# Shared expert of four more blocks made behind a recurrence, and a fourth buffer for the context's tiles

## The chip, the cores and the metric

The kernel runs on one NeuronCore of a Trainium2 chip. The metric is the device time of one execution in microseconds (us). In what follows PE is TensorE (matmuls; PEld its weight loads), DVE is VectorE, ACT is ScalarE, POOL is GpSimd and SP is SyncE, which here only issues DMAs. All data is float32 unless said otherwise. A line number such as L109 is a line of the kernel before the change.

## The reference, cut to what matters

A block of four layers is computed over 16 sequences of 128 tokens with 256 features. Each layer is a mixing step with a residual and a feed-forward step with a residual. The change lies in layer 1:

```python
def step(carry, xs):                  # L1 mixing: a scan over the 128 positions
    r, state = carry
    qt, kt, vt = xs
    r = decay * r + kt * vt
    inp = (qt * r).reshape(B, D) @ Wi.T + bi
    gate = sigmoid(inp @ Wg.T + bg)
    blended = gate * state + (1.0 - gate) * inp
    state = tanh(blended @ A.T + inp @ Bm.T)
    return (r, state), state @ Wo.T + bo

def _moe_forward(x, ...):             # L1 feed-forward, on the layer norm of x
    probs = softmax(x @ router_w.T)   # 64 experts, 8 of them for each token
    ...                               # at most 128 tokens for each expert
    gu = x @ ws_gate_up               # the shared expert, for every token
    sg, su = gu[:, :SF], gu[:, SF:]   # SF = 192
    return routed + silu(sg) * su @ ws_down
```

The next layer's mixing steps need gates, keys and values of a second tensor, the context (`ctx_1024`, 16 x 128 x 256).

## The kernel before, in words

The program has four stretches. Layer 0 comes first (`l0_xattn`, `l0_rest`). Then `l1_steps` runs the recurrence of layer 1, one step for each of the 128 positions. Then `l1_ffn` runs the 64 routed experts in 32 pairs (`l1_experts`). Last, `l2_l3` runs layers 2 and 3.

**A step of the recurrence** is a chain through four engines: PE adds `pre` and 8 small products of `gate` with `wA` (both fp32, so 8 and 16 records in the profile) into a PSUM bank, ACT takes the tanh (`th`, L954), DVE transposes it into `state` (L956) and multiplies the next step's `gate` with it (L959), and PE goes on.

**Work beside the recurrence** fills the engines' idle time. `spread` is a small planner written by hand: it lays chains of parts, each with an engine, a cost in us and a due step, into the 128 steps, so that no engine gets more than `room` allows in one step. In the order of their rights these chains are:

- `l1_block(q)`, first list: for block q, which is 16 positions (two tiles of 128 tokens): the output product, residual, layer norm (`h`), the transposed features `ht` (`even`, L1087), the router, the eight best experts (`best`, `chosen`, `differ`) and sorting keys (`turn_chosen`, `keys`). Block q can begin at step 16q + 16. Block 7 comes behind the last step.
- `l1_early`: the first half of the search for each expert's tokens, on DVE.
- `side_work`: eight pairs of context tiles (`pair(p)`, begin at step 1 + 8p) are loaded by `ctx_pair` into buffers of the tag `c`, of which there are three, and become keys, values (`kvt`) and centred values (`va`, on POOL, L297) for the later layers; four groups become gates. Buffers rotate: the load of pair p waits until POOL has read the tile of pair p - 3.
- `shared`: the second list of `l1_block(q)`, for q = 0 to 5, six steps before the first list's end at the earliest, laid last of all. It is the shared expert of one block: `widen` (8 matmuls of 256 columns, 16 records), a tanh, two copies on ACT and three products on POOL for the silu, `narrow` (4 matmuls, 8 records), a copy on ACT, and `end` (POOL adds it to `x`, and a DMA writes the sum to `expert_sums[0]`, on SP's queue for q under 4 and on POOL's else).

Parts that the planner puts behind step 127 are issued after the loop, along with block 7, and those not needed for the keys are ordered behind `self.turned`, block 7's `turn_chosen` on PE.

**Behind the recurrence** `l1_ffn` makes the router's weights (`l1_weights`), then the shared expert of blocks 6 and 7 in one go (`l1_shared`: matmuls of 512 columns, a real Silu on ACT), then the rest of the search (`l1_slots`: 16 rounds of `max` and `match_replace` on DVE, L1399 and L1401, then a transpose on PE, L1405, and index arithmetic into `slot_tok`). `l1_experts` gathers each expert's tokens with an indirect DMA on POOL (`xg`, L1261), transposes and multiplies on PE, and adds the weighted result into DRAM with another indirect DMA on POOL (`sum`, L1318). The order of instructions on each engine outside pinned parts comes from a scheduler that works at compile time; on the chip each engine takes them in that order.

**Weights of the experts** lie in slots of 9 KB a partition, one for each pair of experts (1.18 MB by eight DMAs on SP). Fourteen slots are used in turn: `EARLY` = 3 in the pool `keep`, filled during the recurrence; `RING` = 7 in `wring`, whose memory is that of the recurrence's helper pools (`side`, `blocks`) once these are done with; `MORE` = 1 in a pool on the right side; and `OLD` = 3, again in `keep`, where the tables of `l1_tables` (`one`, `two`, `three`) lay before: logits and masks, keys, and the features `ht` of blocks 6 and 7 with the router's and the shared expert's weights.

The lines that the prediction follows:

```python
        shared = [(ends[q] - 6, blocks[q][1]) for q in range(6)]
...
        at = ep % (EARLY + RING + MORE + OLD)
        ring = EARLY <= at < EARLY + RING
        w = self.slot(None if ring else self.more if EARLY <= at < EARLY + RING + MORE else self.keep)
```

Of the kernel before, what the change touches and what calls it, by code (L numbers as in the profile page):

```python
# [9 lines left out]
F32 = mybir.dt.float32  # L10
# [18 lines left out]
NE, TOPK, CAP, F1 = 64, 8, 128, 96  # L29


EARLY, RING, MORE, OLD = 3, 7, 1, 3
AHEAD = 5
SLOT = 2304
ROW = D + NE


# [24 lines left out]
class Kernel:  # L62
# [145 lines left out]
    def side_work(self, pool):  # L208
# [18 lines left out]
        def pair(p):  # L227

            s = {}

            def begin():
                s["c"] = self.ctx_pair(p, 3)
                s["st"] = self.small.tile([P, 2, 6], F32, tag="st", name="st")
                s["mv"] = self.small.tile([P, 2, 2], F32, tag="mv", name="mv")

            def stats(i):
                nc.vector.bn_stats(s["st"][:, i], s["c"][:, i])

            def spread(i):
                nc.vector.bn_aggr(s["mv"][:, i], s["st"][:, i])  # L240
                if i:
                    s["r"] = self.rstd(s["mv"][:, :, 1], 2)

            def shift():
                s["less"] = self.small.tile([P, 2], F32, tag="less", name="less")
                nc.vector.scalar_tensor_tensor(s["less"], s["mv"][:, :, 0], -1.0, s["r"], ALU.mult, ALU.mult)

            def scale(i):
                if not i:
                    s["h"] = pool.tile([P, 2, D], F32, tag="h", name="h")  # L250
                nc.scalar.activation(
                    s["h"][:, i], s["c"][:, i], AF.Identity, bias=s["less"][:, i:i + 1], scale=s["r"][:, i:i + 1]
                )

            def turn():
                for c in range(2):
                    for i in range(2):
                        at = (c * 2 + i) * P
                        self.flip(bank["T"][:, at:at + P], s["h"][:, i, c * P:(c + 1) * P])

            def affine(c):
                if not c:
                    s["ct"] = pool.tile([P, 2, 2 * P], F32, tag="ct", name="ct")
                nc.scalar.activation(
                    s["ct"][:, c], bank["T"][:, c * 2 * P:(c + 1) * 2 * P], AF.Identity,
                    bias=self.pcol("cln_b", c), scale=self.pcol("cln_g", c),
                )

            def keys():
                for c in range(2):  # L270
                    self.mm(bank["K"][:, :2 * P], wk[:, c], s["ct"][:, c], c == 0, c == 1)

            def values():
                for bb in range(2):
                    at = 2 * P + bb * 64
                    for c in range(2):
                        self.mm(
                            bank["K"][:, at:at + 64], s["ct"][:, c, bb * P:(bb + 1) * P], wv[:, c], c == 0, c == 1
                        )

            def keep():
                kvt = pool.tile([P, 3 * P], F32, tag="kvt", name="kvt")
                nc.scalar.copy(kvt, bank["K"][:, :3 * P])
                load(out=self.kvt_d[p], in_=kvt)

            def mean():
                s["heads"] = s["c"].rearrange("p b (h d) -> p (b h) d", h=4)
                s["mean"] = self.small.tile([P, 8], F32, tag="mean", name="mean")
                nc.vector.tensor_reduce(s["mean"], s["heads"], AX.X, ALU.add)

            def share():
                nc.gpsimd.tensor_scalar(s["mean"], s["mean"], 1.0 / 64, None, ALU.mult)

            def less():
                va = pool.tile([P, 2, 4, 65], F32, tag="va", name="va", bufs=2)
                nc.gpsimd.memset(va[:, :, :, 64:65], 1.0)
                nc.gpsimd.tensor_tensor(  # L297
                    va[:, :, :, :64].rearrange("p b h d -> p (b h) d"), s["heads"],
                    s["mean"].unsqueeze(2).to_broadcast([P, 8, 64]), ALU.subtract,
                )  # L300
                load(out=self.va_d[p // 2, :, p % 2 * 2:p % 2 * 2 + 2], in_=va)

            return [
                ("SP", 0, begin, 5), ("DVE", 0.5, lambda: stats(0), 0), ("DVE", 0.5, lambda: stats(1), 0),
                ("DVE", 0.2, lambda: spread(0), 0), ("DVE", 0.4, lambda: spread(1), 2), ("DVE", 0.2, shift, 0),
                ("ACT", 0.55, lambda: scale(0), 0), ("ACT", 0.55, lambda: scale(1), 0), ("PE", 0.45, turn, 0, "+T"),
                ("ACT", 0.57, lambda: affine(0), 0), ("ACT", 0.57, lambda: affine(1), 0, "-T"),
                ("PE", 0.86, keys, 0, "+K"), ("PE", 0.45, values, 0), ("ACT", 0.5, keep, 0, "-K"),
                ("DVE", 0.7, mean, 0), ("POOL", 0.4, share, 0), ("POOL", 1.4, less, 0),
            ]  # L310
# [604 lines left out]
    def l1_steps(self, pool, rec, side, last_used):  # L915
# [13 lines left out]
        blocks = [self.l1_block(last_used, q) for q in range(8)]  # L929
        urgent = [(16 * q + 16, blocks[q][0], True) for q in range(7)]  # L930
        out, ends = self.spread(urgent)
        shared = [(ends[q] - 6, blocks[q][1]) for q in range(6)]
        search = [(ends[3] + 1, self.l1_early())]
        beside, _ = self.spread(urgent + search + self.side_work(side) + shared)

# [52 lines left out]
    def l1_tables(self):  # L988
# [8 lines left out]
        w["best"], w["keys"] = two[:, :P], two[:, :5 * P]  # L997
        w["early"], w["iota"] = two[:, 5 * P:9 * P], two[:, 9 * P:17 * P]
        w["val"] = two[:, 17 * P:].rearrange("p (t k) -> p t k", t=NB)
        w["ht"] = three[:, :1024].rearrange("p (c n) -> p c n", c=2)  # L1000
        w["router"] = three[:, 1024:1152].rearrange("p (c n) -> p c n", c=2)
        w["sgu"] = three[:, 1152:1920].rearrange("p (c n) -> p c n", c=2)
        w["sd"] = self.keep.tile([F1, 2, D], F32, name="wsd", bufs=1)
# [20 lines left out]
    def l1_block(self, pool, q):  # L1024
# [55 lines left out]
                    self.flip(bank["T"][:, at:at + P], s["h"][:, h, c * P:(c + 1) * P])  # L1080

        def even():
            if q < 6:
                s["ht"] = pool.tile([P, 2, 2 * P], F32, tag="htb", name="ht", bufs=3)
            else:
                s["ht"] = w["ht"][:, :, (q - 6) * 2 * P:(q - 5) * 2 * P]
            nc.scalar.copy(s["ht"], bank["T"].rearrange("p (c n) -> p c n", c=2))  # L1087

        def router():
# [55 lines left out]

        def end():
            nc.gpsimd.tensor_tensor(xs, xs, s["out"].rearrange("p (h d) -> p h d", h=2), ALU.add)
            queue = nc.sync if q < 4 else nc.gpsimd
            queue.dma_start(out=self.block_rows(self.expert_sums[0], q), in_=xs)

        return [
            ("POOL", 1.3, bias, 0), ("ACT", 0.57, lambda: begin(0), 0), ("ACT", 0.57, lambda: begin(1), 0), ("PE", 0.86, lambda: out(0), 0, "+A"),
# [34 lines left out]
    def l1_ffn(self):  # L1187

        self.right.close()
        with self.tc.issue_after(self.ring_dma.ins):
            self.open_late()
        self.more = self.open(self.mids, "more", MORE, side="right")
        with (
            self.tc.tile_pool(name="l1h", bufs=2, reuse_waits="tile") as hidden,
            self.tc.tile_pool(name="l1r", bufs=1, reuse_waits="tile") as scratch,
        ):
            self.l1_weights(scratch)  # L1200

            with self.tc.issue_after(self.turned.ins):
                self.l1_shared(hidden)
            slot_tok = self.l1_slots(scratch)
        self.l1_experts(slot_tok, self.rows, self.expert_sums)
        self.sums = self.expert_sums
# [16 lines left out]
    def l1_fetch(self, ep):  # L1223

        nc, ins = self.nc, self.ins
        at = ep % (EARLY + RING + MORE + OLD)
        ring = EARLY <= at < EARLY + RING
        w = self.slot(None if ring else self.more if EARLY <= at < EARLY + RING + MORE else self.keep)
        wgu = w[:, :16 * F1].rearrange("p (j c n) -> p j c n", j=2, c=2)
        wd = w[:, 16 * F1:16 * F1 + 2 * D].rearrange("p (j d) -> p j d", j=2)  # L1230
        wt = w[:, 16 * F1 + 2 * D:]
# [113 lines left out]
    def l1_shared(self, pool):  # L1345

        nc, w = self.nc, self.l0
        act = pool.tile([F1, 2, GT], F32, tag="act", name="act")
        for f in range(2):
            pg, pu = self.psum("mm"), self.psum("mm")  # L1350
            for ps, at in ((pg, f), (pu, f + 2)):
                for c in range(2):

                    self.mm(ps[:F1], w["sgu"][:, c, at * F1:(at + 1) * F1], w["ht"][:, c], c == 0, c == 1)
            nc.scalar.activation(act[:, f], pg[:F1], AF.Silu)
            up = pool.tile([F1, GT], F32, tag="up", name="up")
            nc.scalar.copy(up, pu[:F1])
            nc.gpsimd.tensor_tensor(act[:, f], act[:, f], up, ALU.mult)
        for q in (6, 7):
            po = self.psum("mm")  # L1360
            for h in range(2):
                at = ((q - 6) * 2 + h) * P
                for f in range(2):
                    self.mm(po[:, h * D:(h + 1) * D], act[:, f, at:at + P], w["sd"][:, f], f == 0, f == 1)
            xs = self.x[:, q:q + 9:8]
            o = pool.tile([P, 2, D], F32, tag="o", name="o")
            nc.scalar.copy(o.rearrange("p i d -> p (i d)"), po)
            nc.gpsimd.tensor_tensor(xs, xs, o, ALU.add)
            nc.gpsimd.dma_start(out=self.block_rows(self.expert_sums[0], q), in_=xs)

    def l1_weights(self, scratch):

# [846 lines left out]
```

## Time and profile before

| what | value |
|---|---|
| median of 3 runs | 1703.3 us (1701.97 to 1705.75) |
| the profiled execution's own time | 1708.4 us |
| its span, from first to last instruction | 1706.7 us |
| mean granted TensorE clock | 0.945 |
| PE busy | 1527.6 us, 90% |
| DVE busy | 916.3 us, 54% |
| ACT busy | 744.6 us, 44% |
| POOL busy | 465.7 us, 27% |
| recurrence, first tanh to last | 616.3 to 817.4 us |
| search on DVE behind it | 832.6 to 861.6 us |
| first and last gather, last scatter of the experts | 866.4, 1061.6 and 1084.0 us (starts) |

The shares are averages over stretches with different limits, so each stretch has to be read by itself. Times of rows are counted from the span's start. "Granted clock" is the share of full speed that the throttle gave TensorE.

### The profile page before, as it was taken

The page shows a single profiled execution, that of the slowest core. Times are in us where ns is not written, and L with a number is a line of the kernel's source. Part 1 is how long each engine was busy: PE and PEld are TensorE (multiplying, and loading weights), DVE is VectorE, ACT ScalarE, POOL GpSimd, SP SyncE. Part 2 cuts the span into 40 slices and gives each one's busy share as a digit, 9 for nine tenths or more (in the row PEclk, how much of TensorE's full clock was granted, in tenths as well). Part 3 has the DMA queues.
Part 4 walks back from the last instruction along what each step waited for, and adds up shares of the span by engine and source line. Part 5 has one row for each costly group of instructions (what it writes and reads, how often), then busy time and mean ns, then how long its engine had stood idle before and what let it go on. Part 6 is the DMA issues. An engine that isn't in the chain of part 4 may idle for free.

```text
span 1706.7 us, 30312 instructions
## 1 busy us (share of the span) xinstructions
PE 1527.6 (90%) x11743; PEld 1083.7 (63%) x11743; DVE 916.3 (54%) x2410; ACT 744.6 (44%) x2178; POOL 465.7 (27%) x454
## 2 busy tenths in 40 slices
PE   7999999999999988888749889248999999999998
PEld 5777776765444446655437667136777777777776
DVE  4555464556466634557733323367675665765632
ACT  1443343344434223433313323135656756756555
POOL 2001000002122321232547888411421421402211
PEclk9999999999999977999779999668999999999999
DMA  8000000100001112342379997750000100100000
GB/s 260 7 7 7 7 1 1 50 13 23 0 13 38 62 41 86 118 157 72 105 216 285 294 306 154 186 196 16 23 29 19 27 24 27 30 12 8 7 7 13
DMA packets 89120, 125.76 MB, mean 74 GB/s; under 512 B 17936, under 2 KB 65872, under 8 KB 88848
## 3 DMA queue, kind: packets, MB, share of 16 engines
q1 hardware_dynamic: 75024, 101.76, 18.8%
q0 software_dynamic: 12832, 20.72, 5.9%
q8 instruction: 93, 1.52, 0.4%
q10 hardware_dynamic: 1120, 1.34, 0.2%
q14 instruction: 51, 0.42, 0.1%
HBM read 95.21 MB, written 28.57 MB: 73 GB/s over the span
## 4 chain that ended last, share of the span: by engine, by line
PE 66%; DVE 15%; issue 7%; POOL 4%; ACT 3%; DMA 3%; another core or an unknown queue 1%; ACTq 0%; SPq 0%; POOLq 0%; DVEq 0%
PE ps_all L109 43%; PE ps_mm L109 12%; PE ps_av L109 2%; PE ps_sc L109 2%; POOL rstd L161 1%; PE ps_all L1998 1%; PE ps_tp L419 1%; PE ps_all L1570 1%; DVE st L1548 1%; DVE gate L959 1%; DVE h L1553 1%; PE ps_all L1271 1%; DVE state L956 1%; ACT e L408 1%
## 5 line engine op out<-in xcount | busy, mean ns | idle before, releaser
L161 POOL TENSOR_TENSOR rstd<-ve,nhalf 128x2 f32<-128x2 f32 (+1 forms) x81 | 60.4, 749 | 585.9 <-DVE ve L159 500.1
L1990 POOL TENSOR_TENSOR e<-e,rs 128x512 f32<-128x512 f32 x64 | 66.1, 1040 | 282.6 <-DVE rs L1989 266.9
L408 ACT ACTIVATE e<-ps_sc,nmax 128x128 f32<-128x128 f32 x256 | 89.9, 377 | 108.0 <-DVE nmax L404 108.0
L109 PE MATMUL ps_all<-xt,w 128*64 128x128 f32 (+1 forms) x1024 | 104.8, 290 | 18.2 <-DVE xt L120 8.1
L109 PEld LDWEIGHTS ps_all<-xt,w 128*64 128x64 f32 (+1 forms) x1024 | 92.9, 173 | 33.0 <-issue 12.0
L1318 POOL DMA_INDIRECT sum<-y,slot_tok x64 | 102.2, 1596 | 32.5 <-issue 14.5
L1987 ACT ACTIVATE e<-e,nmax 128x128 f32<-128x128 f32 x256 | 99.3, 391 | 12.1 <-DVE nmax L1978 11.5
L954 ACT ACTIVATE th<-ps_all 128x64 f32<-128x64 f32 x128 | 28.6, 223 | 128.6 <-PE ps_all L109 128.1
L956 DVE STREAM_TRANSPOSE state<-th 128x64 f32<-128x64 f32 x128 | 31.3, 245 | 83.4 <-ACT th L954 82.2
L109 PE MATMUL ps_all<-wA,gate 128*16 128x64 f32 x2032 | 61.9, 241 | 15.3 <-DVE gate L959 13.6
L1570 PE MATMUL ps_all<-ident,h 128*128 128x128 f32 x168 | 29.1, 299 | 47.3 <-DVE h L1553 36.5
L1261 POOL DMA_INDIRECT xg<-rows,slot_tok x64 | 63.5, 993 | 26.4 <-issue 13.7
L109 PE MATMUL ps_mm<-ht,wq 128*128 128x256 f32 x256 | 69.7, 396 | 0.0
L109 PE MATMUL ps_mm<-ctxt,wk 128*128 128x256 f32 x256 | 66.9, 385 | 0.0
L109 PE MATMUL ps_mm<-wu,mt 128*128 128x256 f32 x256 | 66.0, 391 | 0.0
L109 PE MATMUL ps_all<-ht,w3q 128*128 128x256 f32 x256 | 61.9, 391 | 0.7 <-ACT ht L1941 0.7
L165 DVE TENSOR_TENSOR x<-x,ps_all 128x256 f32<-128x256 f32 x32 | 13.3, 416 | 89.7 <-PE ps_all L109 89.7
L1553 DVE TENSOR_SCALAR h<-x,mv,rstd 128x256 f32<-128x256 f32 x112 | 45.5, 435 | 29.8 <-POOL rstd L161 29.1
L109 PE MATMUL ps_all<-ht,w3v 128*128 128x256 f32 x256 | 60.9, 381 | 0.0
L109 PE MATMUL ps_all<-ht,w3g 128*128 128x256 f32 x256 | 60.5, 379 | 0.0
L1570 PEld LDWEIGHTS ps_all<-ident,h 128*128 128x128 f32 x168 | 19.8, 148 | 63.1 <-DVE h L1553 31.0
L109 PEld LDWEIGHTS ps_all<-wA,gate 128*16 128x16 f32 x2032 | 38.4, 104 | 33.8 <-DVE gate L959 30.9
(390 smaller groups left out, 3767.3 us busy)
## 6 DMA issues: line engine op xcount, KB each, us to landing
w<-in_moe_gate_up SPq DMA_DIRECT2D x64, 384.0 KB
w<-in_moe_down SPq DMA_DIRECT2D x64, 96.0 KB
c_in<-in_ctx SPq DMA_DIRECT2D x16, 256.0 KB
sum<-zero SPq DMA_DIRECT2D x8, 512.0 KB
w<-in_moe_down SPq DMA_DIRECT2D x64, 64.0 KB
ysum<-sum SPq DMA_DIRECT2D x16, 256.0 KB
low<-tops SPq DMA_DIRECT2D x12, 256.0 KB
va_d<-va SPq DMA_DIRECT2D x8, 260.0 KB
```

Source lines behind the costliest of these rows:

```text
L109: i = self.nc.tensor.matmul(out, lhsT, rhs, start=start, stop=stop)
L161: nc.gpsimd.tensor_tensor(r, ve, self.nhalf[:, :n], ALU.pow)
L408: nc.scalar.activation(e[:, i], src[:, i], AF.Exp, bias=nmax[:, i:i + 1], accum_out=ssum[:, i:i + 1])
L419: self.nc.tensor.transpose(pt[:, i * P:(i + 1) * P], e[:, i], self.ident)
L954: tanh = nc.scalar.activation(th, ps[:, :64], AF.Tanh)
L956: nc.vector.transpose(state[:, :, at:at + 32], th.rearrange("p (c n) -> p c n", c=2))
L1261: nc.gpsimd.indirect_dma_start(out=x, out_offset=None, in_=rows, in_offset=bass.IndirectOffsetOnAxis(ap=slot_tok[:, e:e + 1], axis=0),)
L1318: nc.gpsimd.indirect_dma_start(out=sums[e % len(sums)], out_offset=bass.IndirectOffsetOnAxis(ap=slot_tok[:, e:e + 1], axis=0), in_=y, in_o ...
L1553: nc.vector.tensor_scalar(h[:, i], src[:, i], mv[:, i, 0:1], r[:, i:i + 1], ALU.subtract, ALU.mult)
L1570: self.nc.tensor.transpose(pt[:, at:at + P], h[:, i, c * P:(c + 1) * P], self.ident)
L1987: nc.scalar.activation(e[:, i], e[:, i], AF.Exp, bias=nmax[:, i:i + 1], accum_out=ssum[:, i:i + 1])
L1990: nc.gpsimd.tensor_tensor(e, e, rs.unsqueeze(2).to_broadcast([P, 4, P]), ALU.mult)
```

## The change

The shared expert stays beside the recurrence for blocks 0 and 1 alone (`BESIDE` = 2). Blocks 2 to 7 keep their features `ht` on chip, in pairs of blocks: blocks 2 and 3 and blocks 4 and 5 in a new table `four`, blocks 6 and 7 in `three` as before. `l1_shared` then makes the shared expert of the three pairs one after the other behind block 7, with the same instructions as before for one pair. Their sums are written by DMAs of POOL's queue. The table `four` takes a slot in `keep`, which becomes the slot of a pair of experts later: `OLD` goes from 3 to 4 and `MORE` with its pool goes away, so there are fourteen slots as before. The tag `c` of the context's tiles gets a fourth buffer.

```diff
-EARLY, RING, MORE, OLD = 3, 7, 1, 3
+EARLY, RING, OLD = 3, 7, 4
+BESIDE = 2
...
-                s["c"] = self.ctx_pair(p, 3)
+                s["c"] = self.ctx_pair(p, 4)
...
-        shared = [(ends[q] - 6, blocks[q][1]) for q in range(6)]
+        shared = [(ends[q] - 6, blocks[q][1]) for q in range(BESIDE)]
...
-        w["ht"] = three[:, :1024].rearrange("p (c n) -> p c n", c=2)
+        four = self.slot(self.keep)
+        w["hts"] = [t.rearrange("p (c n) -> p c n", c=2) for t in (four[:, :1024], four[:, 1024:2048], three[:, :1024])]
...
-            if q < 6:
+            if q < BESIDE:
                 s["ht"] = pool.tile([P, 2, 2 * P], F32, tag="htb", name="ht", bufs=3)
             else:
-                s["ht"] = w["ht"][:, :, (q - 6) * 2 * P:(q - 5) * 2 * P]
+                at = q % 2 * 2 * P
+                s["ht"] = w["hts"][(q - BESIDE) // 2][:, :, at:at + 2 * P]
...
-            queue = nc.sync if q < 4 else nc.gpsimd
-            queue.dma_start(out=self.block_rows(self.expert_sums[0], q), in_=xs)
+            nc.sync.dma_start(out=self.block_rows(self.expert_sums[0], q), in_=xs)
...
-        self.more = self.open(self.mids, "more", MORE, side="right")
...
-        at = ep % (EARLY + RING + MORE + OLD)
+        at = ep % (EARLY + RING + OLD)
-        w = self.slot(None if ring else self.more if EARLY <= at < EARLY + RING + MORE else self.keep)
+        w = self.slot(None if ring else self.keep)
...
     def l1_shared(self, pool):
-        act = pool.tile([F1, 2, GT], F32, tag="act", name="act")
-        for f in range(2):
+        for n, ht in enumerate(w["hts"]):
+            act = pool.tile([F1, 2, GT], F32, tag="act", name="act")
+            for f in range(2):
...
-        for q in (6, 7):
+            for q in (BESIDE + 2 * n, BESIDE + 2 * n + 1):
...
```

More of the change, by code (lines that the diff above doesn't have):

```diff
@@ L1347, in l1_shared @@
         nc, w = self.nc, self.l0
-        act = pool.tile([F1, 2, GT], F32, tag="act", name="act")
-        for f in range(2):
[L1350 to L1358, printed above, removed]
@@ L1359, in l1_shared @@
-        for q in (6, 7):
[L1360 to L1369, printed above, removed]
+        for n, ht in enumerate(w["hts"]):
+            act = pool.tile([F1, 2, GT], F32, tag="act", name="act")
+            for f in range(2):
+                pg, pu = self.psum("mm"), self.psum("mm")
+                for ps, at in ((pg, f), (pu, f + 2)):
+                    for c in range(2):
+                        self.mm(ps[:F1], w["sgu"][:, c, at * F1:(at + 1) * F1], ht[:, c], c == 0, c == 1)
+                nc.scalar.activation(act[:, f], pg[:F1], AF.Silu)
+                up = pool.tile([F1, GT], F32, tag="up", name="up")
+                nc.scalar.copy(up, pu[:F1])
+                nc.gpsimd.tensor_tensor(act[:, f], act[:, f], up, ALU.mult)
+            for q in (BESIDE + 2 * n, BESIDE + 2 * n + 1):
+                po = self.psum("mm")
+                for h in range(2):
+                    at = (q % 2 * 2 + h) * P
+                    for f in range(2):
+                        self.mm(po[:, h * D:(h + 1) * D], act[:, f, at:at + P], w["sd"][:, f], f == 0, f == 1)
+                xs = self.x[:, q:q + 9:8]
+                o = pool.tile([P, 2, D], F32, tag="o", name="o")
+                nc.scalar.copy(o.rearrange("p i d -> p (i d)"), po)
+                nc.gpsimd.tensor_tensor(xs, xs, o, ALU.add)
+                nc.gpsimd.dma_start(out=self.block_rows(self.expert_sums[0], q), in_=xs)
```

## The prediction

> **What bounds the kernel now.** I read the page's chain first, then the four stretches that the change touches. A difference under 0.2% (3.4 us) is about what a measurement of this kernel can't tell from none.
>
> The recurrence. The tile view of `th` gives its ends: 127 intervals in 201.1 us, 1.58 on average. The timeline of ACT's tanh gives single steps: a bare step takes 1.27 us, one with a burst of four records of the shared expert 1.49 to 1.53. The windows view has the clock of three stretches of it:
>
> ```profile
> L954 ACT ACTIVATE th<-ps_all x128: 223/223/224, 616.3 to 817.4; 128x64 f32<-128x64 f32 x128
> ```
> ```profile
> core 0: us, PE busy (x) PEld busy (x) DVE busy (x) ACT busy (x) POOL busy (x), PEclk, DMA share, GB/s
> 616.00:619.00 3.00, 1.77 (x56) 0.89 (x56) 0.88 (x4) 0.66 (x3) 0.00 (x0) 1.00 0.00 0
> 619.00:638.00 19.00, 13.80 (x329) 7.09 (x329) 6.78 (x33) 3.71 (x15) 0.72 (x1) 0.51 0.01 3
> ...
> 768.00:813.00 45.00, 39.08 (x868) 24.93 (x866) 33.96 (x127) 15.39 (x55) 12.25 (x11) 1.00 0.21 68
> ...
> 858.00:878.00 20.00, 5.10 (x19) 3.91 (x20) 6.36 (x19) 0.00 (x0) 9.76 (x12) 0.51 0.97 288
> ```
>
> The number behind POOL's is the granted clock (PEclk): half in 619 to 638, where almost nothing runs beside the steps, full in 768 to 813, where bursts do. The last row has the DMA engines at 0.97 while the first tokens are gathered.
>
> The chain of waits, in the recurrence and behind it:
>
> ```profile
> 715.12 1.05 POOL va L297
> 716.19 5.67 DMA c_in<-in_ctx
> 721.89 0.75 DVE st L237 x2
> ...
> 858.97 0.84 DVE top L1399
> 859.84 0.90 DVE key L1401 x2
> 860.75 0.84 DVE top L1399
> 861.73 0.46 PE ps_all L1405
> ...
> 864.63 19.27 another core or an unknown queue
> ```
>
> The eighth context tile is loaded only when POOL has read the fifth, and DVE, which the recurrence needs, stands still for its landing. Behind the recurrence the search on DVE is the chain to L1405. Then comes a piece whose releaser the trace doesn't name. SP's waits and the timeline say what lies there:
>
> ```profile
> SPq L1234 <- POOL x L1147: 23.0, 1, 23.0
> ```
> ```profile
> 846.27 3.60 PE L109 MATMUL ps_all<-w 128*96 128x512 f32 x8
> ...
> 852.29 2.86 PE L109 MATMUL ps_all<-wsd,act 96*128 96x256 f32 x12 [0.85 <-POOL act L1358]
> ...
> 866.39 1.07 POOL L1261 DMA_INDIRECT xg<-rows,slot_tok  x1 [7.20 <-DMA w<-in_moe_down]
> ...
> 883.92 0.38 ACT L1296 ACTIVATE a<-ps_all 128x256 f32<-128x256 f32 x1 [28.15 <-remote]
> ...
> 892.56 1.64 POOL L1318 DMA_INDIRECT sum<-y,slot_tok  x1 [11.31 <-DVE y L1317]
> ```
>
> SP held the third and later ring slots for 23 us, until block 5's shared expert was added at 849.0; the rest of the weights came at 849 to 881, over the gathers. PE's matmuls for pair 0 end by 880.1 and its next transposes at 880.6, yet ACT gets them at 883.9. From 892.6 to 1085.5 POOL is the bound: 64 scatters at 1.58 + 0.3 and 52 gathers at 0.98 + 0.3 make 187 of 193 us. So the expert stage ends a fixed time after its first scatter, and what moves that moves the end.
>
> **The change part by part.**
>
> *Fourth buffer.* The load of tile 7 then waits for tile 3, read at 696.4, and can land by about 712, seven us before DVE asks. The interval of tanh 65 to 66 is 3.97 us, its neighbours 1.5: -2.5 us (bounds -1.5, if something else is late next, and -3.0, DVE's whole wait). No other load is in the chain.
>
> *Shared expert out of the recurrence.* The shared chains are laid last, so taking some away moves nothing else. The tiles `act` and `ht` show where they ran: blocks 0 and 1 at 681 to 770, which stay; blocks 2 and 3 and the widening of block 4 at 748 to 816; block 4's narrowing and nearly all of block 5 behind the recurrence already. So only steps 80 to 127 change. They lose 12 widening and 4 narrowing bursts of 0.86 us of PE, each of which stretched a step from 1.27 to about 1.51: 16 x 0.24 = -3.8 us. ACT's 0.6 us parts and POOL's 1.27 us products go with them; they lie beside.
>
> Against it stands the clock. In the row 619 to 638 the bare steps 3 to 12 take 1.48 us, 0.21 more than bare steps at full clock. From step 95 on (block 1's shared expert ends at 770) only blocks 5 and 6 with one chain each are left on PE, some 33 steps. If half of them fall to half clock: 33 x 0.5 x 0.21 = +3.5; none 0, all +6.9. The Trainium skill (TensorE: Matmul & The Clock Gate, "HAM oscillation — how this bites in real kernels") asks only that PE have no idle gaps over some 3.4 us. A step has none near that long, so by the rule the clock stays full and this part is -3.8. But the row has half clock in just such a stretch, with PE busy 13.8 of 19 us. The trace decides: I take -3.8 + 3.5 = -0.3, bounds -3.8 and +3.1.
>
> *Shared expert in the tail.* By the two matmul rows a 512-column record takes 3.60 / 8 = 0.45 us, a 256-column one 2.86 / 12 = 0.24. A pair of blocks has 16 of each: 11.0 us; three pairs 33 us. They may start behind `turned` at 831.9, where the clock is half until about 838 (up to 3 us more): PE ends at 865 to 868. L1405 stood at 861.7 with PE idle for 6.6 us before it; now it is 3 to 6 us late if the scheduler puts it behind all of them, and 0 to 2 if it slips in ahead of the last narrowing (16 x 0.24 = 3.8). I take +3.0, bounds 0 and +7.5. POOL was busy 22.2 of 34.7 us from 831.7 to 866.4; it loses 8.1 (blocks 4 and 5) and gets 4 x 1.28 products, 4 x 1.27 additions and 4 DMA issues at 1.05 with their gap, 14.4. That is 28.5 of 34.7: hidden, unless the last additions come behind PE's end; two of them with their DMAs are 4.6 us ahead of the gathers, which the same +3.0 and its upper bound cover. ACT gets 3.5 us a pair in 34 us with 20 idle. SP loses two issues of 0.4.
>
> *Weights earlier.* `up` and `act` of the blocks' pool are then last used at 771, so the third slot's wait on L1147 goes; late next is block 7's `h`, read by PE and by a DMA at 827 to 830. The ten remaining loads of the ring at 2.2 to 2.6 us each are done by about 855, ahead of the gathers. What stands to go: the 3.5 us between PE's last transpose at 880.4 and ACT at 883.9, and some of the 5.95 us from the first gather to PE's transpose at 872.34. The first gap's cause isn't named in the trace; the weight traffic at 0.97 is its neighbour. I take -4.0, bounds 0 (loads into the table slots come over the gathers instead) and -5.5.
>
> *Slots.* Pair 10 takes table `one`, free once the router's weights are written (issued 846.5), needed at 939: 80 us of cover, so 0; if that went, its 1.18 MB at 288 GB/s cost 4 us once.
>
> Sum: -2.5 - 0.3 + 3.0 - 4.0 = -3.8. The profiled execution took 1708.4 (its span and 1.7 around it), so 1704.6; it lies 5.1 above the median, and the same step from that gives 1699.5.
>
> **The rivals.**
>
> *PE becomes the bound of the tail* (slower). PE's 33 us start 3 us slow at half clock, and the last narrowing waits 2.5 us for ACT and POOL, so L1405 stands at 868.4 or the last additions hold the gathers till 873.9: +7.5. The loads into `two`, `three` and `four` then begin as the gathers do, and only 2 us of the first pair's loss go. With a cold recurrence: -2.5 + 3.1 + 7.5 - 2.0 = +6.1: 1709.4. It decides once the gathers are some 6 us later, seen from the last tanh. For it: PE's work ends beyond 861.7 by any count. Against: the scheduler can put L1405 between.
>
> *All of it pays.* L1405 finds a gap, the clock stays full, the DMA queues are empty at the gathers: -2.5 - 3.8 - 5.5 = -11.8: 1691.5. For it: search and shared expert use different engines. Against: the 0.51 row.
>
> *The weights gain nothing* (the change doesn't do what it could): -2.5 - 0.3 + 3.0 = +0.2: 1703.5. For it: the gap's cause is not in the trace.
>
> **How the numbers follow.** Forecast 0.42 (its own range 1695.5 to 1703.5: 0.22 faster, 0.19 same, 0.01 slower), PE-bound tail 0.32 (0.30 slower, 0.02 same), all pays 0.17 (faster), no gain from the weights 0.09 (0.06 same, 0.03 slower). Faster 0.39, same 0.27, slower 0.34. The range 1692 to 1711 leaves out half of the case in which all pays and a third of the slow one.
>
> **What would show it.** No wait of DVE L237 on the load of `c_in`, and no tanh interval near 4 us. Tanh intervals from step 95: 1.27 if the clock holds, 1.48 if not. SP's 23 us wait on L1147 gone and the ring's loads done by 860. L1405 against the last tanh: 44.3 us now; 47 by the forecast, 51 by the rival. From first gather to first scatter: 26.2 us now, about 22 forecast. I am wrong if the stage from first scatter to last doesn't keep its 193 us.

## The result, and the profile after

The changed kernel took 1718.3 us (median of 4 runs, 1710.9 to 1722.5) against 1702.7 (4 runs): ratio 1.0089, 95% interval 1.0062 to 1.0116. Measured again beside experiments it took 1711.5 (12 runs, 1706.9 to 1717.4) against 1704.4: ratio 1.0050 (1.0032 to 1.0067). It is slower; 1699.5 had been predicted. The profiled execution (1710.9 us, span 1709.2) is the fastest of its four, and that of the second measurement (1706.9) the fastest of its twelve, so the profiles show less than the median loss. The times of the four follow the mean granted clock: 0.939, 0.933, 0.931 and 0.928 for 1710.9, 1716.2, 1720.5 and 1722.5 us.

Lines of the changed kernel stand one to three above those of the kernel before (L955 is the tanh, L957 `state`, L960 `gate`, L1408 the search's transpose). The tile view of `th` and three windows:

```profile
L955 ACT ACTIVATE th<-ps_all x128: 223/223/225, 612.5 to 818.2; 128x64 f32<-128x64 f32 x128
```
```profile
core 0: us, PE busy (x) PEld busy (x) DVE busy (x) ACT busy (x) POOL busy (x), PEclk, DMA share, GB/s
615.00:634.00 19.00, 13.54 (x327) 7.02 (x328) 6.78 (x33) 3.88 (x15) 0.72 (x1) 0.52 0.08 27
765.00:803.00 38.00, 31.48 (x525) 19.43 (x528) 21.98 (x88) 7.70 (x32) 0.71 (x1) 0.56 0.15 45
803.00:824.00 21.00, 15.43 (x278) 9.47 (x271) 14.38 (x50) 4.40 (x16) 1.19 (x3) 0.59 0.34 104
```

The recurrence takes 205.7 us where it took 201.1. The granted clock is 0.56 from 765 to 803, where the kernel before had 1.00 (its row from 768 to 813).

Behind the recurrence, the timeline of the kernel before (first) and of the changed one shows the last transpose of the search, the next matmul (`back`), and DVE's conversion into `tok`:

```profile
861.73 0.45 PE L1405 MATMUL ps_all<-ident,top 128*128 128x128 f32 x1 [6.58 <-DVE top L1399]
...
862.65 0.66 PE L109 MATMUL ps_all<-lists,back 128*128 128x64 f32 x2 [0.48 <-DVE lists L1407]
...
864.38 0.20 DVE L1418 CAST tok<-slot 128x64 int32<-128x64 f32 x1
```
```profile
864.82 0.27 PE L1408 MATMUL ps_all<-ident,top 128*128 128x128 f32 x1
...
866.18 2.86 PE L110 MATMUL ps_all<-wsd,act 96*128 96x256 f32 x12 [1.09 <-POOL act L1361]
...
868.87 0.33 PE L110 MATMUL ps_all<-lists,back 128*128 128x64 f32 x2
...
870.05 0.75 POOL L1372 DMA_DIRECT2D sum<-x  x1 [0.30 <-POOL x L1371]
870.33 1.83 DVE L1421 CAST tok<-slot 128x64 int32<-128x64 f32 x1
870.83 1.27 POOL L1371 TENSOR_TENSOR x<-x,o 128x512 f32<-128x512 f32 x1
...
873.98 1.07 POOL L1263 DMA_INDIRECT xg<-rows,slot_tok  x1 [0.86 <-DMA gbias<-in_pcols]
...
883.66 0.38 ACT L1298 ACTIVATE a<-ps_all 128x256 f32<-128x256 f32 x1 [13.95 <-PE ps_all L110]
```

The transpose finds a gap on PE, but `back` then stands behind narrowing matmuls of the shared expert, and the conversion ends only when POOL's addition does. ACT's first activation for pair 0 comes 9.7 us after the first gather (873.98); before, it came 17.5 us after (866.39 and 883.92).

All of it as a ledger, worked out from the starts of `th`, `slot_tok`, gathers and scatters in the two profiles ("again" is the profile of the second measurement, span 1705.2):

| stretch | before | after | again | after - before |
|---|---|---|---|---|
| start to first tanh | 616.3 | 612.5 | 613.3 | -3.8 |
| tanh 0 to 64 | 103.4 | 99.9 | 101.8 | -3.5 |
| tanh 64 to 67 (fourth buffer) | 7.6 | 5.2 | 5.2 | -2.4 |
| tanh 67 to 80 | 22.3 | 21.5 | 23.6 | -0.8 |
| tanh 80 to 127 | 67.9 | 79.0 | 73.6 | +11.1 |
| last tanh to L1405 / L1408 | 44.3 | 46.6 | 45.8 | +2.3 |
| from there to first gather | 4.7 | 9.2 | 9.2 | +4.5 |
| first gather to first scatter | 26.2 | 18.7 | 18.7 | -7.5 |
| first to last scatter | 191.4 | 191.4 | 191.9 | 0.0 |
| last scatter to end | 622.7 | 625.1 | 622.3 | +2.4 |

The first two rows, the row from tanh 67 to 80 and the last are left out: hardly any of the shared expert was taken from these stretches (one burst, at 748), and they vary between executions (the two profiles of the changed kernel differ by 1.9, 2.1 and 2.8 us in the last three of them). So the change itself reads -2.4 + 11.1 + 6.8 - 7.5, or +8.0; by the second profile -2.4 + 5.7 + 6.0 - 7.5, or +1.8. The kernel before has a single profile.

### The profile page after: what moved, and what is told of

Same layout as the page of the kernel before. It is cut to its first block, busy times and chain, and to the rows that moved or that the text cites. A ratio compares the mean times of both kernels' runs of the same rounds, so it can differ in the third digit from the quotient of the medians.

```text
span 1709.2 us, 30227 instructions
## 1 busy us (share of the span) xinstructions
PE 1536.7 (90%) x11700; PEld 1082.4 (63%) x11711; DVE 918.4 (54%) x2410; ACT 744.3 (44%) x2174; POOL 457.7 (27%) x448
## 3 DMA queue, kind: packets, MB, share of 16 engines
q1 hardware_dynamic: 74480, 101.23, 18.7%
## 4 chain that ended last, share of the span: by engine, by line
PE 65%; DVE 13%; issue 7%; DMA 7%; POOL 4%; ACT 3%; ACTq 0%; SPq 0%; POOLq 0%; DVEq 0%
PE ps_all L110 42%; PE ps_mm L110 12%; DMA xg<-rows,slot_tok 2%; PE ps_av L110 2%; DMA w<-in_moe_gate_up 2%; PE ps_sc L110 2%; POOL rstd L162 1%; PE ps_all L2001 1%; DVE gate L960 1%; PE ps_tp L420 1%; DMA sum<-y,slot_tok 1%; PE ps_all L1573 1%; DVE st L1551 1%; DVE state L957 1%; DVE h L1556 1%
## 5 line engine op out<-in xcount | busy, mean ns | idle before, releaser
L955 ACT ACTIVATE th<-ps_all 128x64 f32<-128x64 f32 x128 | 28.6, 223 | 138.7 <-PE ps_all L110 135.0
L957 DVE STREAM_TRANSPOSE state<-th 128x64 f32<-128x64 f32 x128 | 31.4, 245 | 92.2 <-ACT th L955 91.6
L110 PE MATMUL ps_all<-wA,gate 128*16 128x64 f32 x2032 | 65.9, 255 | 14.9 <-DVE gate L960 12.1
L110 PE MATMUL ps_all<-ident,pre 128*16 128x64 f32 x1024 | 43.3, 247 | 20.7 <-ACT th L955 19.8
```

Of the source, the lines that this page charges most:

```text
L110: i = self.nc.tensor.matmul(out, lhsT, rhs, start=start, stop=stop)
L955: tanh = nc.scalar.activation(th, ps[:, :64], AF.Tanh)
L957: nc.vector.transpose(state[:, :, at:at + 32], th.rearrange("p (c n) -> p c n", c=2))
```

## The experiments

Ratios are to the kernel before, run on the same chip. Its median lay between 1702.7 and 1710.3 us in the different groups of runs, so kernels of different groups are compared by their ratios. Times of stretches are from each run's profile, one for each kernel.

**The fourth buffer alone.** In the kernel before:

```diff
-                s["c"] = self.ctx_pair(p, 3)
+                s["c"] = self.ctx_pair(p, 4)
```

> The kernel before with the fourth context buffer alone. Theory (the buffer is worth what the prediction said): the tanh interval of 3.97 us goes to about 1.5, 2.5 us off: about 1700.2. Rival (another wait takes its place in the recurrence): no change, 1702.7.

1706.1 us, ratio 1.000 (0.998 to 1.002). Tanh 64 to 67 takes 5.2 us instead of 7.6. The 2.4 us are there, and they are 0.14%, which the ratio can't show. First gather to first scatter stays at 27.0.

**Idle matmuls late in the recurrence.** The changed kernel with one idle matmul in each step from 78 on, its result not used:

```diff
+            if s >= 78 and s + 1 < P:
+                ...
+                    self.mm(self.bank["D"][:, :D], self.ident, w["Wo"][:, 0])
```

> The kernel after, with one fp32 matmul of 256 columns into a free PSUM bank (its result is not used) in each step from 78 on. Clock theory (the loss is half clock in steps 80 to 127, where the block chains then cost twice): TensorE stays at full clock, the 47 intervals from tanh 80 on go from 81.6 us to about 66 to 70, and the time falls from 1718 to 1700 to 1706. Tail theory (the loss is PE and POOL behind the recurrence, gathers 7.6 us later): the steps get no shorter or the time stays above 1714.

1709.8 us, ratio 1.0019 (1.0006 to 1.0032). The windows of this kernel:

```profile
741.00:800.00 59.00, 58.26 (x1084) 38.36 (x1087) 38.88 (x152) 15.01 (x59) 5.26 (x6) 1.00 0.35 111
800.00:812.00 12.00, 11.81 (x254) 6.67 (x245) 9.45 (x37) 3.01 (x12) 0.70 (x1) 1.00 0.15 41
```

The clock is full, and steps 80 to 127 take 70.1 us instead of 73.6 and 79.0. More work on PE made them shorter. The total is above the 1700 to 1706 us expected, because first gather to first scatter was 25.6 us here and 18.7 in the changed kernel: a stall that comes up again below.

**The tail's shared expert left out.** The changed kernel without the shared expert of blocks 2 to 5; their sums are written without it.

```diff
-        for n, ht in enumerate(w["hts"]):
+        for n, ht in list(enumerate(w["hts"]))[2:]:
```

> The kernel after, with the shared expert of blocks 2 to 5 left out of the computation (their rows are still written). Tail theory: the gathers come 7 us earlier after the last tanh, the first scatter too, and the time falls to 1703 or lower, since the tail is the whole loss. Clock theory: the gathers come earlier by the same 7 us, but steps 80 to 127 stay at about 81 us or more, so the time stays at 1709 to 1713.

1714.8 us, ratio 1.0043 (1.0027 to 1.0058). `slot_tok` comes 48.8 us after the last tanh, against 54.7 and 53.9 in the two profiles with it and 47.9 before: the tail's share is 5 to 6 us. The time hardly shows it, as the steps from 80 on are still slow (73.1 us) and the stall is here too (26.1).

**Everything but the move.** The changed kernel with the shared expert of blocks 0 to 5 beside the recurrence again, its sums on the queues of before. Its tiles `act` and `up` move to `keep`, so the ring's memory is still free early; the ring has 6 slots.

```diff
-EARLY, RING, OLD = 3, 7, 4
+EARLY, RING, OLD = 3, 6, 4
...
-        shared = [(ends[q] - 6, blocks[q][1]) for q in range(BESIDE)]
+        shared = [(ends[q] - 6, blocks[q][1]) for q in range(6)]
...
-            s["act"] = pool.tile([F1, 2, 2 * P], F32, tag="act", name="act")
+            s["act"] = self.keep.tile([F1, 2, 2 * P], F32, tag="act", name="act", bufs=2)
```

> The kernel after, with the shared expert of blocks 2 to 5 back beside the recurrence, but its helper tiles (act, up) in the tables' pool, so that no slot of the ring waits for them; one ring slot fewer to make room. Clock theory: steps 80 to 127 as before the change (about 69 us from tanh 80), gathers as before the change, weights early as after it, so the first scatter comes about 7 us earlier than before the change: about 1693. If the early weights gained nothing of their own: 1700.

1701.6 us, ratio 0.9968 (0.9956 to 0.9979). Steps 80 to 127 take 69.5 us, the first gather comes 48.4 us after the last tanh. So the move of the shared expert is what costs, and the rest of the change pays 0.3%. Of that the profile shows 2.4 us at the fourth buffer; the early weights gained little here, as first gather to first scatter takes 25.6 us.

**The changed kernel again**, unchanged, beside the next runs.

> The changed kernel once more, to have a second profile of it and its time beside the next kernels on one chip. Clock theory: about 0.9% above the kernel before, and the profile again has steps 80 to 127 at 75 us or more with half clock in several windows of it. If the stretch is back at 68 to 70 us and the time is still above, the clock is not the cause.

The numbers stand above; 0.5% and 73.6 us from step 80 on are less than the 0.9% and 75 us expected, but half clock is there again. The windows of its profile:

```profile
781.00:801.00 20.00, 15.87 (x287) 9.43 (x280) 12.56 (x49) 4.92 (x19) 0.71 (x1) 0.50 0.05 15
801.00:808.00 7.00, 5.17 (x150) 3.07 (x149) 4.61 (x20) 1.11 (x5) 0.00 (x0) 0.98 0.01 2
```

PE is busy for 79% of the first row at half clock and for 74% of the second at full clock. The same steps fell to half clock at other places than in the first profile (733 to 753, 781 to 801 and 808 to 822 here; 732 to 735, 742 to 749, 766 to 776, 779 to 803 and 807 to 824 there), which goes with the wide spread of this kernel's times.

**Shared expert beside, and idle matmuls in every light step.** The kernel of "everything but the move" with:

```diff
+            if 0 < s < P - 1 and self.used.get((s, "PE"), 0.0) < 0.3:
+                ...
+                    self.mm(sums[(s + 1) % 2][:, 256:512], self.ident, w["Wo"][:, 0])
```

> The kernel with the shared expert back beside the recurrence and the ring freed, plus one fp32 matmul of 256 columns (unused result, spare columns of the steps' own banks) in every step that the planner gave less than 0.3 us of PE. Clock theory: the half-clock windows of the recurrence go (bare steps 3 to 15 from 1.48 to 1.27), 5 to 9 us less than without the filler: ratio to before about 0.992. Rival (a filler matmul costs the step as much as the clock gives): the same 0.997 as without it, or slower.

1688.2 us, ratio 0.9906 (0.9878 to 0.9934). The bare steps 3 to 12 take 1.27 us instead of 1.48, tanh 0 to 24 31.9 us instead of 35.1, and the last tanh comes at 803.2.

**Fewer gathers at the start.** The kernel of "everything but the move", fetching 3 pairs ahead instead of 6:

```diff
+            for ep in range(3):
+                fetch(ep)
...
+                    if ep + 2 < pairs:
+                        fetch(ep + 2)
```

> The kernel with the shared expert back beside the recurrence and the ring freed, with tokens gathered for 3 pairs of experts instead of 6 ahead of the first. In five of six profiles PE's results reach ACT only some 17 us after the first gather, whether weights are loading or not; that is when the twelve gathers have landed. If the burst of gathers holds PE up, the second silu comes by 12 us and the first scatter some 5 us earlier after the first gather (20 instead of 25.6): ratio to before about 0.994. If not, 17 us and 25.6 stay, and the time stays at 0.997.

1695.2 us, ratio 0.9946 (0.9926 to 0.9967); first gather to first scatter 19.0 us instead of 25.6. It looked as if the burst of gathers made the stall. But the kernel before it in this list has the full burst and 18.4 us.

**The search first.** The changed kernel with `l1_slots` written ahead of `l1_shared`:

> The changed kernel with l1_slots called ahead of l1_shared, so that the scheduler prefers the search's transpose, matmul and arithmetic where both are ready. Tail theory: the first gather comes back from 55 us to about 49 or 50 behind the last tanh, and the time falls by 4 to 6 us against the changed kernel of the same chip; if the shared expert's matmuls still stand between, 55 stays.

1746.0 us, ratio 1.0225 (1.019 to 1.026), a miss. `slot_tok` came 49.3 us after the last tanh, but the first gather 86.8. POOL's timeline shows why:

```profile
877.99 1.25 POOL L1361 TENSOR_TENSOR act<-act,up 96x512 f32<-96x512 f32 x1 [25.87 <-ACT up L1360]
...
911.81 1.08 POOL L1263 DMA_INDIRECT xg<-rows,slot_tok  x1 [0.39 <-DMA flat<-in_L_ffn_w_gateT]
```

The shared expert of the three pairs ran behind the search, and its last addition and DMA stand just ahead of the first gather in POOL's order (909.1 and 910.7). It also shows its price when the search doesn't cover it: 37 us from `slot_tok` to the first gather.

**The changed kernel with idle matmuls in every light step**, the same lines as above.

> The changed kernel with one idle matmul of 256 columns in every step of the recurrence whose planned work on PE is under 0.3 us; its result is not used. Clock theory (the change lost its time because steps 80 to 127 fell to half clock): steps 80 to 127 fall from 73.6 to 79.0 us to about 69, steps 0 to 24 from 35.1 to about 32, the first gather stays 55 us after the last tanh, and the ratio to the kernel before comes to about 0.997 (0.994 to 1.000). Tail theory (most of the loss is the late gather): the steps gain nothing by it, and the ratio stays at 1.005 or above.

1694.1 us (10 runs), ratio 0.9955 (0.9942 to 0.9969). The window:

```profile
737.00:801.00 64.00, 62.76 (x1257) 38.17 (x1260) 46.88 (x184) 17.69 (x69) 5.95 (x7) 1.00 0.34 109
```

Steps 80 to 127 take 64.6 us: 3.3 fewer than before the change, where I had put 3.8 for the bursts taken out. The loss of 0.5 to 0.9% turned into a gain by work whose result is thrown away. The search's end is as late as before (`slot_tok` +54.4).

**The kernel before with idle matmuls**, nothing else changed:

> The kernel before with the same idle matmuls, nothing else changed. Clock theory: only the bare steps near the start gain, steps 0 to 24 from 35.1 to about 32, steps 80 to 127 stay at 68 to 70: ratio about 0.998 (0.993 if the 7 us stall between first gather and first scatter happens to go). If idle matmuls only stretch the chain: 1.000 to 1.003. It also tells how much of the gain of 0.94% of the kernel with shared work beside and idle matmuls is due to the idle matmuls alone.

1690.0 us (4 runs), ratio 0.9929 (0.9904 to 0.9954). Tanh 0 to 24 takes 31.9 us, steps 80 to 127 68.1. So idle matmuls alone bring most of what the best kernel has. Not all of that is the clock: 5.3 us of it lie between first gather and first scatter (20.9 instead of 26.2), where the stall has gone. And with idle matmuls in both, the change still shows no gain: 1694.1 against 1690.0. Its steps are 3.5 us shorter, its gathers 6.8 us later (55.5 against 48.7 after the last tanh), and gathers to scatters 2.3 us shorter (18.6 against 20.9). That makes +1.0 of the +4.1 between the medians; the two profiled executions stand the other way round (1688.4 and 1693.5), mainly through the stretches behind the first scatter. In this kernel tanh 64 to 67 takes 5.2 us too, with three buffers. The eighth context tile on its timeline:

```profile
705.61 1.04 POOL L297 TENSOR_TENSOR va<-c_in,mean 128x512 f32<-128x512 f32 x1
...
706.68 0.54 SPq L1567 DMA_DIRECT2D c_in<-in_ctx  x1
...
709.70 0.75 DVE L237 BATCH_NORM_STATS2 st<-c_in 128x6 f32<-128x256 f32 x2 [0.34 <-DMA c_in<-in_ctx]
```

The load still waits for POOL's `va`, but lands within 3.0 us instead of 5.7, and DVE waits 0.34. What the fourth buffer saved was a slow load, not a wait that is always there.

**Four more matmuls at the start.** The kernel of "everything but the move", with idle matmuls in steps 4 to 7 only:

```diff
+            if 3 < s < 8:
```

> The kernel with the shared expert beside the recurrence and the ring freed, plus idle matmuls in steps 4 to 7 only. It asks about the stall of ACT behind the first gathers (completions of PE reach ACT only some 17 us after the first gather; first gather to first scatter 25.6 us with it, 18.5 without). If the stall hangs on where PE's instructions lie in its stream, four matmuls more at the start can move or remove it: 18 to 19 us. If it hangs on the transfers or the order of work in the tail, which are unchanged, it stays at 25 to 26 us.

1695.5 us in one run, where the kernel before took 1702.7 (1701.6 without the four, but there the kernel before took 1707.9, so most of the 6 us is not theirs). First gather to first scatter 18.5 us instead of 25.6. ACT's first rows behind the gathers, without the four (first) and with them:

```profile
872.10 0.38 ACT L1299 ACTIVATE a<-ps_all 128x256 f32<-128x256 f32 x1 [21.99 <-issue]
878.46 0.28 ACT L1301 ACTIVATE a<-ps_all 128x128 f32<-128x128 f32 x1 [5.98 <-remote]
```
```profile
871.18 0.38 ACT L1305 ACTIVATE a<-ps_all 128x256 f32<-128x256 f32 x1 [20.77 <-PE ps_all L110]
872.79 0.28 ACT L1307 ACTIVATE a<-ps_all 128x128 f32<-128x128 f32 x1 [1.23 <-PE ps_all L110]
```

The wait of 5.98 us with an unnamed releaser is gone, though neither the gathers nor the weights nor the number of transfers changed.

**Two pairs behind the recurrence instead of three.** The changed kernel with idle matmuls and:

```diff
-BESIDE = 2
+BESIDE = 4
```

> The changed kernel with idle matmuls, but the shared expert of blocks 2 and 3 back beside the recurrence, so that two pairs of blocks are left for the tail instead of three. Theory (the tail pays 6.8 us because PE has about 37 us of the third pair's and the others' work to issue ahead of the search's last matmul, while two pairs end before the search does): slot_tok ends 48 to 49 us after the last tanh instead of 54.4, steps 80 to 127 take 65.5 to 67 us instead of 64.6, first gather to first scatter stays 18.5 us if the stall stays away; ratio to the kernel before 0.991 to 0.994. Rival (the lateness comes with POOL's and DVE's sharing and not with PE's amount of work): slot_tok stays at 53 or later and the ratio at 0.995 or above.

1696.1 us, ratio 0.9921 (0.9894 to 0.9949). `slot_tok` comes 49.3 us after the last tanh; steps 80 to 127 take 67.1 us.

```profile
849.73 0.66 PE L110 MATMUL ps_all<-lists,back 128*128 128x64 f32 x2 [0.48 <-DVE lists L1416]
...
851.46 0.20 DVE L1427 CAST tok<-slot 128x64 int32<-128x64 f32 x1
```

PE's work for two pairs ends before the search does, so `back` waits for nothing on PE, and POOL's additions are over when the conversion runs (its last DMA for them began at 846.4). The stall came back (first gather to first scatter 26.4 us), though nothing in the tail but the amount of shared work differs; without it this kernel might stand some 7 us lower, which was not shown.

The three fastest kernels (ratios 0.9906, 0.9921 and 0.9929) have overlapping intervals. All three beat both kernels of this study, and all three have idle matmuls.

## Why the prediction was wrong

*Fourth buffer, -2.5:* right against the one profile of the kernel before, -2.4 in every kernel with four buffers. That three buffers cost these 2.4 us only while the load takes 5.7 us was not in it, and how often the kernel before has so slow a load is not known.

*Shared expert out of the recurrence, -0.3 (at most +3.1):* this is the step that failed; it measured +11.1 in one profile and +5.7 in the other. The direction of the mechanism was right, and the gain of 3.8 too (3.3 with the clock held). Mis-sized was the term "33 x 0.5 x 0.21", +3.5. Against the same steps with the clock held, those from 95 on cost 11.8 and 5.8 us in the two profiles, and those from 80 to 95, which I had put at nothing, 2.7 and 3.2. The share of half clock was low by a part: 46 of 54 us from step 95 on in the first profile and 30 of 48 in the second, where I took half. The price was low by more, since even all 33 steps at 0.21 make only 6.9. I took it from bare steps, and bare steps do pay 0.21 (1.27 to 1.48, steps 107 and 108). But every sixteen steps some carry the output product or the router's product of blocks 4 to 6, and these I left at their old length. Timeline of the kernel before, then of the changed one:

```profile
775.83 0.22 ACT L954 ACTIVATE th<-ps_all 128x64 f32<-128x64 f32 x1 [0.60 <-PE ps_all L109]
...
777.10 1.13 PE L109 MATMUL ps_all<-wWo,st 128*128 128x256 f32 x4
777.29 0.22 ACT L954 ACTIVATE th<-ps_all 128x64 f32<-128x64 f32 x1 [1.23 <-PE ps_all L109]
```
```profile
770.66 2.07 PE L110 MATMUL ps_all<-wWo,st 128*128 128x256 f32 x4
770.86 0.22 ACT L955 ACTIVATE th<-ps_all 128x64 f32<-128x64 f32 x1 [1.31 <-PE ps_all L110]
...
773.23 2.08 PE L110 MATMUL ps_all<-wWo,st 128*128 128x256 f32 x4
773.42 0.22 ACT L955 ACTIVATE th<-ps_all 128x64 f32<-128x64 f32 x1 [2.34 <-PE ps_all L110]
...
776.20 0.22 ACT L955 ACTIVATE th<-ps_all 128x64 f32<-128x64 f32 x1 [2.56 <-PE ps_all L110]
```

Four records of the output product take 2.07 us instead of 1.13, and they stand in PE's order ahead of the next step, so the steps take 2.56 and 2.78 us instead of 1.53 and 1.52. Eight such steps (83, 84, 98, 100, 101, 114, 116, 117) lost 9.0 of the 11.1 us, and 4.0 of the 5.7 in the second profile.

The rule of the Trainium skill that I had weighed (TensorE: Matmul & The Clock Gate, "HAM oscillation — how this bites in real kernels"), idle gaps of some 3.4 us, would by my reading have kept the clock full and this part at -3.8. In steps 98 to 102 of the changed kernel the longest idle time before a row of PE or of its weight loads is 0.67 us, and the clock in the windows above was 0.50 to 0.59. The measurement decides: the clock fell with no gap near 3.4 us, and with idle matmuls in the light steps it was 1.00 (the windows from 741 and from 737 above).

*Shared expert in the tail, +3.0 (0 to +7.5):* +6.8 and +6.0, inside the bounds, by another way. L1405 was only 2.3 us late; the gap that I had hoped for was there. I had not followed the chain behind it: `back` is a matmul too and stood behind the last narrowing (+3.1 us, 0.92 to 4.05 from transpose to `back`), and `tok` met POOL's addition (+1.6). The run with two pairs took back 5.1 of it.

*Weights earlier, -4.0 (0 to -5.5):* -7.5, beyond the bound, and mostly by luck. The ring's wait on `x` was gone and its last load issued at 851 (855 forecast). The three kernels that have idle matmuls in all light steps and no stall put the worth of that at 2.3 to 2.5 us (20.9 with late weights, 18.6 and 18.4 with early ones). The other 5 us were the unnamed gap, and that is not the weights' doing: four kernels with early weights have it (25.6 twice, 26.1, 26.4) and the kernel before with idle matmuls, with late weights, has not. "The first gap's cause isn't named in the trace; the weight traffic at 0.97 is its neighbour" was the weak point, and neighbourhood was no cause.

*Slots, 0, and the 193 us from first to last scatter:* right; the stage took 189 to 194 us in every kernel.

The rival of the PE-bound tail foresaw the sign and nearly the size of the tail, not the clock's: it had +3.1 where the runs had +5.7 to +11.1. By the ledger's terms the sum is -2.4 + 11.1 + 6.8 - 7.5 = +8.0, or 1711.3 from the median shown of before; the first measurement's median lies 7 us above even that, at mean clocks near 0.93, where its profiled execution had 0.939. No profile shows where these 7 us lie.

## What to carry to other kernels

Price a lower clock by the busiest steps of a stretch, not by its bare ones: they hold the matmuls that nearly double (1.13 to 2.07 us here). Before taking work away from a matmul engine that runs in short steps, ask whether that work holds its clock; if it does, idle matmuls in the light steps are cheap to try, and here they brought more than the change. Where work is put beside a chain on other engines, follow that chain to its last instruction, since every later matmul or conversion of it can meet the work again.

## What the runs showed of the hardware

- Steps with PE busy for 70 to 80% ran at half or at full clock in turn, in places that differ between executions of the same program (0.50 from 781 to 801 and 0.98 from 801 to 808 in one profile). In the windows with idle matmuls PE was busy for 98 to 99% and the clock was 1.00. The busy share alone doesn't tell the clock: in the changed kernel PE was busy for all of 742 to 749, at 0.52, and matmuls take longer at half clock (2.07 us for four records instead of 1.13).
- In 60 runs of the kernel before, time and mean granted clock went together: about -1.06 us for +0.001 (correlation -0.77).
- A stall of 5 to 7 us behind the first gathers comes and goes with the program: in the kernel before, in the fourth buffer's, in three with early weights and in the one with two pairs; not in the changed kernel (two profiles) nor in six others. In the six kernels that have it, it ended 16.8 to 17.5 us after the first gather. Four matmuls added some 240 us earlier removed it. Weights, the burst of gathers and the order in the tail are ruled out as its sole cause; where instructions lie in the program is one thing left, but no run shows that by itself, and every kernel but the changed one has a single profile. One instruction transfer (queue q8) falls between first gather and first scatter both in "everything but the move", which has the stall, and in the changed kernel, which has not, so its presence alone doesn't decide. The cause stays open.
- A small DVE conversion took 1.83 us instead of 0.20 in four profiles (the changed kernel's two and two with idle matmuls). In each it began 0.5 us ahead of a POOL addition, while POOL issued a DMA, and ended as the addition did. Whether the DMA's issue or the addition held it is not shown.
